# Reordering the start of a fused attention and deformable-convolution kernel, with a finer split at each image's border

## The chip, the cores and the metric

The kernel runs on one core of one Trainium2 chip. The metric is the device time of the whole program in microseconds, the median of the runs shown. One execution was also taken by the hardware profiler; every duration of one instruction below comes from that execution.

## The reference

The input `x` has 8 images of 256 channels by 64 by 64 pixels, all in 32-bit floats. Two residual layers follow each other, each on a group norm with 32 groups of 8 channels.

```
x = x + L0(gn(x))      # local attention over 3x3 windows
x = x + L1(gn(x))      # modulated deformable 3x3 convolution

L0: q, k, v = w_qkv @ x;  attn = softmax over the 9 neighbours of q.k (4 heads)
    kernel = w_kg @ (q, k, v) + b_kg              # 9 weights a pixel and head
    out = w_proj @ (alpha * sum(kernel * v_patch) + beta * sum(attn * v_patch))
L1: om = conv3x3(x, w_off) + b_off                # 18 offsets and 9 masks a pixel
    for each of 9 taps: sample x bilinearly at the shifted point (4 corners),
    times sigmoid(mask), then multiply by the tap's 256x256 weight and add up
```

## The kernel before

**Chunks, slots and halves.** An image is worked on in 8 chunks of 8 rows (512 pixels); 256 channels are two halves of 128 partitions. The kernel has two kinds of work. The *front* of an image is its first layer and the preparation of its second: `attention(b)` makes q, k, v, the logits, softmax, weighted sums and projection chunk by chunk, then `prepare(b)` norms the result, writes it to a table in DRAM whose row holds a pixel and its lower neighbour (`to_table`), and computes the offsets (`Offsets`: 18 products of 32 columns, four of them side by side, for one chunk), their transposes (`turn`) and from them row numbers and weights (`positions`). The *sampling* of an image then takes 72 slots, one for each chunk and tap. A slot has four blocks of 128 pixels. For each block GpSimd issues an indirect DMA (`gather`, line 1092) that brings 128 rows of 4 KB; ScalarE scales the first corner (`scale`, line 1108); VectorE adds the other three (`sum_corners`, line 1116, in pairs of blocks); TensorE transposes the blocks (line 1146), ScalarE copies them to SBUF (line 1149), and TensorE multiplies by the tap's weight (line 1171).

**What sets the order.** The instructions of TensorE, ScalarE, VectorE and GpSimd are written out by hand: they run in the order of the program text. The front is a Python generator, and each `next(steps)` writes out one step of it; 144 steps (`STEPS`) make an image. In the main loop each slot is issued in two halves, with one step of the next image's front after each half. So the first image's front runs with nothing beside it, the fronts of images 1 to 7 lie between the samplings of images 0 to 6, and the sampling of the last image has no front beside it. `STEPS_AHEAD = 12` says how far the front leads when sampling begins; the start-up code hands out these 12 steps one by one between the first gathers:

```
for n in range(4): next(steps, None)
for i in range(6): gather(i)
next(steps, None); scale(0); scale(1)
next(steps, None); sum_corners(0)
for i in range(6, LEAD, 2):        # LEAD = 16 blocks
    next(steps, None)
    ...                            # gathers 6 to 15, a few scales and sums between
next(steps, None)
```

**Buffers.** Gathered blocks have 10 buffers (`GATHERS`), and a gather waits until the sum has read the buffer's last block. Products of the front go through 4 PSUM buffers in turn (`psum_a`). So a product waits until ScalarE or VectorE has read what lies in its buffer; the logits' products (`products`, line 394) are read by `masked` on VectorE (line 407), and v's products follow them in the same four buffers.

**The start.** The first image's 8 chunks, `w_qkv` in two parts, and the small `w_kgT` are loaded by the queues of SP and ScalarE. TensorE makes from the last two the folded weight (`folded`, line 225), VectorE takes the statistics of each chunk (line 299) and collects them (line 192). Then `fold` scales the folded weight on VectorE (lines 237 and 244). The norm (`Norm`) has two steps: `means` is a product with `gmat` (line 197) and four small VectorE instructions, `ready` a second product (line 208), a square root on ScalarE, and two more. Only then can VectorE norm the chunk (`normed`, line 269) and TensorE make q (line 320).

**The border of two images.** At the end of `prepare(b)` the offsets of chunk 6 (`six`) are made in three parts, products 0 to 5, 6 to 11 and 12 to 17. The next image's `attention` begins with `means`, then `ready`, then its first jobs, of which the first is `turn(six)`.

Of the kernel before, what the change touches and what calls it, by code (L numbers as in the profile page):

```python
# [9 lines left out]
F32 = mybir.dt.float32  # L10
# [7 lines left out]
P = 128  # L18
C = 256
NT = C // P  # L20
# [6 lines left out]
NC = H // R  # L27
KK = 9
# [18 lines left out]
SUM_AHEAD = 6  # L47
SCALE_AHEAD = SUM_AHEAD + 2
GATHERS = 10
LEAD = SUM_AHEAD + GATHERS  # L50
STEPS = 2 * SLOTS
STEPS_AHEAD = 12

@with_exitstack
def preact_kernel(ctx: ExitStack, tc: tile.TileContext, a: dict, out: bass.AP):
# [30 lines left out]
    def load_chunk(b, c, queue=nc.sync):  # L88
        s = slice(c * N, (c + 1) * N)
        queue.dma_start(image[:, :, s], sources[b][:, :, s])  # L90
# [8 lines left out]
    gp = ctx.enter_context(tc.tile_pool(name="gp", bufs=GATHERS))  # L99
    w_qkv = [gp.tile([96, 4, C], F32, tag="g", name=f"w_qkv{i}") for i in range(2)]  # L100
    w_kgT = gp.tile([96, 8, KK], F32, tag="g", name="w_kgT")
    queues = nc.sync, nc.scalar
    for c in range(4):
        load_chunk(0, c, queues[c % 2])
    for i in range(2):
        queues[i].dma_start(w_qkv[i], a["w_qkv"][:, 4 * i : 4 * i + 4, :])
    nc.scalar.dma_start(w_kgT, a["w_kgT"])
    for c in range(4, NC):
        load_chunk(0, c, queues[c % 2])
    gmat = const_tile("gmat", [P, P])  # L110
    w_qkvT = const_tile("w_qkvT", [P, NT, 3 * C], nc.sync)
    alpha = const_tile("alpha", [P, 1])
# [68 lines left out]

    def psum_a(name):
        return ps_a.tile([P, 512], F32, tag="a", name=name)

    class Norm:

# [440 lines left out]
    def attention(b):  # L627

        xt = image
        first = b == 0  # L630
        jobs, due[:] = due[:], []
        gn = norm0[b]
        if b != 1:
            gn.means()
        stats = p2.tile([P, NT, NC, 6], F32, tag="stats", name=f"stats1_{b}")
        yield None
        gn = gn.gn if b == 1 else gn.ready()
        yield None
        xn = normed(xt, gn, 0, 2)
        for job in jobs[:1]:  # L640
            job()
        yield None
        d = added = None
        for c in range(NC):
            if c != 1:
                a_ = Attention(b, c, xn, stats)
                a_.q(0)
                if added:
                    added.second_stats()
                if c in (2, 5, 6, 7):  # L650
                    yield None
                a_.q(1)
                yield None if c == 4 else "quiet"
            else:
                a_ = follows
            ahead_of = c + 1 < NC
            at = 2 * (c % 2)
            a_.k(0)
            if ahead_of:
                xn = normed(xt, gn, c + 1, at, cts=(0,))  # L660
            yield None if ahead_of else "quiet"
            a_.k(1)
            if ahead_of:
                normed(xt, gn, c + 1, at, cts=(1,))
            if first:
                for n in (c - 1, c)[: 1 + (c == NC - 1)]:
                    if n >= 0:
                        first_stats(1, n)
            yield None if ahead_of else "quiet"
            if d and not first:  # L670
                d.keys(0)
            a_.products(0)
            for job in jobs[c - 1 : c] * (c in (2, 3)):
                job()
            yield None if c in (2, 3) else "quiet"
            a_.generated()
            a_.masked(0)
            yield None
            a_.products(1)
            a_.turned()  # L680
            yield "quiet"
            if d:
                d.weighted(0)
            else:
                a_.v(0)
            a_.masked(1)
            a_.summed()
            yield None
            a_.logits_1()
            a_.carry_k()  # L690
            if d:
                d.keys(1)
                d.carry_v()
                yield None
                a_.v(0)
                a_.logits_2()
                a_.softmax_1()
                yield None
                d.weighted(1)
                a_.twisted()  # L700
            else:
                a_.v(1)
                a_.logits_2()
                yield None
                a_.softmax_1()
                a_.twisted()
                follows = Attention(b, 1, xn, stats)
                follows.q(0)
            yield None
            if d:  # L710
                a_.v(1)
            else:
                follows.q(1)
            a_.softmax_2()
            a_.softmax_3()
            yield None
            if d:
                d.add(0, d.project(0))
                yield None
            a_.weights()  # L720
            if first and c == NC - 1:
                norm0[1].means()
            if d:
                d.add(1, d.project(1))
                added = d
            yield None
            a_.spread_weights()
            if first and c == NC - 1:
                norm0[1].ready()
            if first:  # L730
                a_.keys(0)
            yield None
            d = a_
        if not first:
            d.keys(0)
        added.second_stats()
        yield None
        d.weighted(0)
        yield "quiet"
        d.keys(1)  # L740
        yield "quiet"
        d.weighted(1)
        yield "quiet"
        if not first:
            later[0]()
        yield "quiet"
        d.add(0, d.project(0))
        d.add(1, d.project(1))
        d.second_stats()
        gn = Norm(stats, f"1_{b}")  # L750
        yield None
        if not first:
            later[1]()
        yield "quiet"
        gn.means()
        yield None
        gn.ready()
        yield gn.gn

    def prepare(b, gn):  # L760
# [199 lines left out]
        def turn(o):  # L960
            pairs[o.c // 2] = o.turned(o.c % 2)
# [11 lines left out]
        if b == 0:  # L973
            flat(1)
            order = (
                "T0 z2 x1 T1 z3 O0 T2 t z4 x2 O1 T3 t z5 p0 T4 z6 x3 O2 T5 t z7 x4 T6 O3 "
                "T7 t x5 O4 x6 t O5 x7 t p2 S0 S1 S2"
            )
            for job in order.split():
                kind, n = job[0], int(job[1:] or 0)  # L980
                if kind == "T":
                    to_table(n)
                elif kind == "z":
                    flat(n)
                elif kind == "x":
                    xn[n] = normed(xt, gn, n, n % 3, (n - 1) % 3)
                    for m in range(n - 1, n + (n == NC - 1)):
                        nc.gpsimd.tensor_copy(image[:, :, m * N : (m + 1) * N], second[m])
                elif kind == "O":
                    o = Offsets(n, xn[n])  # L990
                    o.all()
                elif kind == "t":
                    turn(o)
                elif kind == "p":
                    positions(n, pairs[n // 2], 2)
                elif n == 0:
                    six = Offsets(NC - 2, xn[NC - 2])
                    six.part(0, 6)
                elif n == 1:
                    six.part(6, 12)  # L1000
                else:
                    six.part(12, KK * NT)
            o = Offsets(NC - 1, xn[NC - 1])
            for n in range(2 * NC):
                yield
# [16 lines left out]
        if b > 0:  # L1022
# [15 lines left out]
                first_stats(b + 1, NC - 1)  # L1038
            o = Offsets(NC - 1, xn[NC - 1])
            yield  # L1040
            six.part(12, KK * NT)
        if not more:
            yield
            turn(six)
# [11 lines left out]
            return  # L1056
        later[:] = [o.first, o.rest, o.positions]
        due[:] = [
            lambda: turn(six),
            lambda: positions(4, pairs[2], 2),  # L1060
            lambda: positions(6, pairs[3]),
# [139 lines left out]
        mybir.EngineType.Pool,  # L1201
    }
    with tc.manual_schedule(engines=ordered):
        ps = folded()
        for c in range(NC):
            first_stats(0, c)
# [2 lines left out]
        for n in range(STEPS):  # L1209
            next(steps, None)  # L1210

        for n in range(4):
            next(steps, None)
        for i in range(6):
            gather(i)
        next(steps, None)
        scale(0)
        scale(1)
        next(steps, None)
        sum_corners(0)  # L1220
        for i in range(6, LEAD, 2):
            next(steps, None)
            if holds:
                nc.gpsimd.memset(holds.pop(), 0.0)
            if i == 8 or i == 12:
                sum_corners(i // 2 - 2)
            gather(i)
            gather(i + 1)
            if i in (6, 10, 14):
                scale(i // 2 - 1)  # L1230
                scale(i // 2)
        next(steps, None)
        done = STEPS + STEPS_AHEAD
        last = None
        for n in range(B * SLOTS + 1):
            late, last = last, None
# [2 lines left out]
            for m in range(NT):  # L1239
# [14 lines left out]
                        stored(*last, slice(m, m + 1))  # L1254

                h = NT * n + m + 1
                goal = h * STEPS
                while (done - STEPS - STEPS_AHEAD) * STEPS < goal:
                    state["quiet"] = next(steps, True)
                    done += 1  # L1260
                if n < B * SLOTS:
# [77 lines left out]
```

## Time and profile before

| what | value |
|---|---|
| runs shown | 4606.46, 4612.72, 4614.89 us; median 4612.72 |
| profiled execution: its time, its span | 4635.28 us, 4633.3 us |
| TensorE busy, matmul records | 4480.2 us (97%), 25344 |
| VectorE, ScalarE, GpSimd busy | 4130.8 us (89%), 2514.2 us (54%), 2783.1 us (60%) |
| gathers: records, share of the DMA engines | 2304, 74.4% |

The profiled execution took 22.6 us more than the median of the runs; differences between steps are read inside it. A 32-bit product of 128 by 128 with 512 columns appears as two matmul records. In a row of the timeline the first number is the start in microseconds from the span's start, the second is the time from the group's start to its end, and the bracket says how long the engine had been idle before it and on what it waited. In a row of the windows each engine has its busy microseconds within the stretch; PEclk is the granted TensorE clock as a share of full speed, then come the share of the DMA engines and GB/s.

### The profile page before, as it was taken

The numbers are of one execution on the slowest core, as the hardware profiler recorded it, in microseconds if no ns is written. First come the engines' busy times: TensorE is split into PE (matmuls) and PEld (weight loads), VectorE is DVE, ScalarE is ACT, GpSimd is POOL, SyncE is SP. The second block draws the span as 40 slices with busy tenths as digits, with TensorE's granted clock in tenths as the row PEclk, the third lists the DMA queues.
The fourth block names the chain that finished last, engine by engine and source line by source line (L and its number), as shares of the span: only waits on it lengthen the run. The fifth ranks groups of instructions, "written<-read, shape, count | busy, mean of one in ns | idle before, by whom it ended". The sixth has DMA issues, their size and how long they took to land.

```text
span 4633.3 us, 77608 instructions
## 1 busy us (share of the span) xinstructions
PE 4480.2 (97%) x25344; PEld 2332.3 (50%) x25344; DVE 4130.8 (89%) x10183; ACT 2514.2 (54%) x5280; POOL 2783.1 (60%) x2850
## 2 busy tenths in 40 slices
PE   8989999999999999999999999999999999998888
PEld 4445554555545555455554555555554555543344
DVE  6669999999999999999989999999999999988777
ACT  3345556555565555555555555655556555554444
POOL 0046655666555665566655665556655666568887
PEclk9999999999999999999999999999999999999999
DMA  4078889888998899988899888998899888899998
GB/s 143 28 230 294 304 312 368 314 301 303 310 385 297 294 312 320 369 295 306 301 338 331 298 307 311 354 331 297 299 315 373 296 287 302 296 335 333 352 336 317
DMA packets 445761, 1412.46 MB, mean 305 GB/s; under 512 B 46430, under 2 KB 63070, under 8 KB 445228
## 3 DMA queue, kind: packets, MB, share of 16 engines
q0 software_dynamic: 331776, 1208.11, 74.4%
q1 hardware_dynamic: 111836, 196.82, 11.8%
q8 instruction: 199, 3.26, 0.3%
q10 hardware_dynamic: 1744, 2.59, 0.2%
q14 instruction: 206, 1.69, 0.1%
HBM read 1275.97 MB, written 131.36 MB: 304 GB/s over the span
## 4 chain that ended last, share of the span: by engine, by line
PE 86%; DVE 4%; DMA 4%; issue 2%; POOL 2%; ACT 1%; another core or an unknown queue 0%; POOLq 0%; DVEq 0%; ACTq 0%; SPq 0%
PE po L1171 38%; PE pt L1146 10%; PE psk L351 5%; PE psq L320 5%; PE proj L602 5%; PE psv L351 5%; PE om L838 5%; PE av L586 3%; DVE s L1116 3%; PE vk L568 2%; PE qk L394 2%; DMA g<-table,idx 2%; PE wk L542 2%; PE gen L437 1%; DMA x<-in_x_dram 1%
## 5 line engine op out<-in xcount | busy, mean ns | idle before, releaser
L1092 POOL DMA_INDIRECT g<-table,idx x2304 | 2670.7, 1159 | 1352.4 <-DVE s L1116 409.1
L1116 DVE SCALAR_TENSOR_TENSOR s<-g,wt,s 128x256 f32<-128x256 f32 x6912 | 2822.9, 479 | 185.8 <-ACT s L1108 127.2
L1171 PE MATMUL po<-vt,w_conv 128*128 128x512 f32 x4608 | 2198.1, 602 | 0.4 <-issue 0.3
L1171 PEld LDWEIGHTS po<-vt,w_conv 128*128 128x128 f32 x4608 | 813.9, 192 | 774.8 <-issue 765.4
L1108 ACT ACTIVATE s<-g,wt 128x256 f32<-128x256 f32 x2304 | 1053.5, 511 | 204.8 <-DMA g<-table,idx 133.1
L1149 ACT COPY vt<-pt 128x512 f32<-128x512 f32 x1152 | 618.2, 589 | 456.5 <-PE pt L1146 330.8
L1146 PE MATMUL pt<-ident,s 128*128 128x128 f32 x4608 | 646.1, 280 | 76.4 <-ACT vt L1149 32.5
L1146 PEld LDWEIGHTS pt<-ident,s 128*128 128x128 f32 x4608 | 527.2, 142 | 340.9 <-issue 197.8
L838 PE MATMUL om<-xn,w_off 128*32 128x512 f32 (+1 forms) x2560 | 272.4, 553 | 0.0
L351 PE MATMUL psv<-xn,w_qkvT 128*128 128x512 f32 (+1 forms) x576 | 251.5, 564 | 3.7 <-issue 2.8
L351 PE MATMUL psk<-xn,w_qkvT 128*128 128x512 f32 (+1 forms) x576 | 246.8, 557 | 0.0
L320 PE MATMUL psq<-xn,w_qkvT 128*128 128x512 f32 x512 | 240.6, 600 | 2.8 <-issue 2.5
L602 PE MATMUL proj<-acc,w_projT 128*128 128x512 f32 x512 | 239.6, 593 | 0.7 <-ACT acc L593 0.7
L328 ACT COPY q<-psq 128x512 f32<-128x512 f32 x128 | 74.8, 586 | 234.5 <-PE psq L320 228.4
L407 DVE TENSOR_TENSOR qk<-qk,near_k 128x400 f32<-128x400 f32 x256 | 134.8, 569 | 73.7 <-PE qk L394 36.8
L593 ACT COPY acc<-av 128x512 f32<-128x512 f32 x128 | 74.8, 584 | 227.9 <-PE pt L1146 164.0
L362 ACT COPY k<-psk 128x512 f32<-128x512 f32 (+1 forms) x144 | 79.1, 551 | 202.3 <-PE psk L351 179.7
L586 PEld LDWEIGHTS av<-wk,vk 100*64 100x64 f32 x4096 | 133.0, 137 | 107.2 <-issue 64.1
L838 PEld LDWEIGHTS om<-xn,w_off 128*32 128x32 f32 x2560 | 75.0, 109 | 207.7 <-issue 201.3
L573 ACT COPY vk<-vk 100x512 f32<-100x512 f32 x256 | 138.3, 592 | 62.2 <-PE vk L568 52.8
L550 DVE TENSOR_TENSOR wk<-wk,near 100x512 f32<-100x512 f32 x256 | 158.7, 682 | 12.9 <-PE wk L542 12.8
L586 PE MATMUL av<-wk,vk 100*64 100x64 f32 x4096 | 154.4, 225 | 12.1 <-issue 11.4
(107 smaller groups left out, 3387.6 us busy)
## 6 DMA issues: line engine op xcount, KB each, us to landing
table<-ts SPq DMA_DIRECT2D x128, 384.0 KB
g<-table,idx POOLq DMA_INDIRECT x2304
x<-x SPq DMA_DIRECT2D x56, 512.0 KB
r<-x SPq DMA_DIRECT2D x56, 512.0 KB
out_dram<-r SPq DMA_DIRECT2D x56, 512.0 KB
x<-in_x_dram SPq DMA_DIRECT2D x52, 512.0 KB
table<-ts SPq DMA_DIRECT2D x128, 128.0 KB
second<-in_x_dram SPq DMA_DIRECT2D x8, 512.0 KB
```

Of the source, the lines that this page charges most:

```text
L320: nc.tensor.matmul(ps, w_qkvT[:, ct, m * P : (m + 1) * P], window(self.xn, ct, 4), start=(ct == 0), stop=(ct == NT - 1),)
L351: nc.tensor.matmul(ps[:, : (hi - lo) * W], w_qkvT[:, ct, o : o + P], self.xn[:, ct, lo:hi, 1 : W + 1], start=(ct == 0), stop=(ct == NT - 1),)
L550: nc.vector.tensor_mul(wk.rearrange("p (t n) -> p t n", n=T * T), ps[:NK].rearrange("p (t n) -> p t n", n=T * T), near.unsqueeze(1).to_bro ...
L586: nc.tensor.matmul(av[64 * h : 64 * h + 64, g, t * T * T : (t + 1) * T * T], self.vk[:, t, o : o + 64], self.wk[2 * g + h][:, i * n + t * ...
L602: nc.tensor.matmul(ps, w_projT[:, ct, m * P : (m + 1) * P], self.acc[:, ct].rearrange("p (t y x) -> p y t x", y=T, x=T), start=(ct == 0), ...
L838: nc.tensor.matmul(self.ps[32 * g : 32 * g + 32, cols], w_off[:, ct, k, :], window(self.xn, ct, k)[:, ys], start=(n < 4), stop=(tail >= 0),)
L1092: nc.gpsimd.indirect_dma_start(out=g, out_offset=None, in_=tables[b % 2], in_offset=bass.IndirectOffsetOnAxis(ap=found[b, c][0][:, j, k : ...
L1108: nc.scalar.activation(s, g[:, 0:C], AF.Copy, scale=w[:, 0:1])
L1116: nc.vector.scalar_tensor_tensor(s, g[:, q * C : (q + 1) * C], w[:, q : q + 1], s, ALU.mult, ALU.add)
L1146: nc.tensor.transpose(pt[ct][:, j, :], s[:, ct * P : (ct + 1) * P], ident)
L1149: nc.scalar.copy(v[:, ct, :], pt[ct].rearrange("p b n -> p (b n)"))
L1171: nc.tensor.matmul(po[m], w_conv[:, ct, k, m * P : (m + 1) * P], v[:, ct, :], start=(k == 0 and ct == 0), stop=(b + 1 < B and k == KK - 1 ...
```

## The change

Three things are changed, and one of them has two places.

1. **The start's loads.** `w_kgT` is moved from seventh to third in the order of loads, and both parts of `w_qkv` are put on ScalarE's queue. The order of the first chunks over the two queues changes with that, and the last two chunks no longer have the first loads of other constants ahead of them.
2. **Products of zeros.** A tile `warm` of zeros is multiplied into a PSUM buffer whose content nobody reads: 9 products of 512 columns ahead of `folded`, and 2 between the end of the first image's attention and its second norm.
3. **The lead at the start of sampling.** Sampling begins when the front is 8 steps ahead (`STEPS_FIRST`) instead of 12. Gathers 0 to 9 are issued in a row after the fourth step, without the small memset that held gather 6 back; scales and sums of the first six blocks follow, with four steps between them. In the main loop four extra steps are handed out over the first 144 halves (after halves 1, 37, 73 and 109), so that the lead is 12 from then on.
4. **The border.** For all images but the last, the last three of the 18 offset products of chunk 6, with the copy that follows, are issued after the next image's `means` instead of before it.

```diff
+STEPS_FIRST = 7 + 1
...
-    for c in range(4):
-        load_chunk(0, c, queues[c % 2])
+    load_chunk(0, 0)
+    load_chunk(0, 1, nc.scalar)
+    nc.scalar.dma_start(w_kgT, a["w_kgT"])
+    load_chunk(0, 2)
     for i in range(2):
-        queues[i].dma_start(w_qkv[i], a["w_qkv"][:, 4 * i : 4 * i + 4, :])
-    nc.scalar.dma_start(w_kgT, a["w_kgT"])
-    for c in range(4, NC):
-        load_chunk(0, c, queues[c % 2])
+        nc.scalar.dma_start(w_qkv[i], a["w_qkv"][:, 4 * i : 4 * i + 4, :])
+    load_chunk(0, 3)
+    load_chunk(0, 5)
+    load_chunk(0, 4, nc.scalar)
+    load_chunk(0, 7)
+    load_chunk(0, 6, nc.scalar)
...
+    warm = const.tile([P, 512], F32, name="warm")
+    nc.vector.memset(warm, 0.0)
+    warming = psum_a("warm")
+
+    def kept_warm(n, size=512):
+        for i in range(n):
+            nc.tensor.matmul(
+                warming[:, :size], warm[:, :P], warm[:, :size], start=True, stop=True
+            )
...
+        part, jobs = jobs[:1], jobs[1:]
         gn = norm0[b]
         if b != 1:
             gn.means()
+        for job in part:
+            job()
...
         gn = Norm(stats, f"1_{b}")
+        if first:
+            kept_warm(2)
...
-            six.part(12, KK * NT)
+            six.part(12, 15 if more else KK * NT)
...
         due[:] = [
+            lambda: six.part(15, KK * NT),
             lambda: turn(six),
...
     with tc.manual_schedule(engines=ordered):
+        kept_warm(9)
         ps = folded()
...
-        for n in range(4):
+        for n in range(STEPS_FIRST - 4):
             next(steps, None)
-        for i in range(6):
+        for i in range(GATHERS):
             gather(i)
-        next(steps, None)
-        scale(0)
-        scale(1)
-        next(steps, None)
-        sum_corners(0)
-        for i in range(6, LEAD, 2):
-            next(steps, None)
-            if holds:
-                nc.gpsimd.memset(holds.pop(), 0.0)
-            if i == 8 or i == 12:
-                sum_corners(i // 2 - 2)
-            gather(i)
-            gather(i + 1)
-            if i in (6, 10, 14):
-                scale(i // 2 - 1)
-                scale(i // 2)
-        next(steps, None)
-        done = STEPS + STEPS_AHEAD
+        for i in range(0, SUM_AHEAD, 2):
+            if i == 0:
+                scale(0)
+                scale(1)
+            scale(i + 2)
+            scale(i + 3)
+            sum_corners(i)
+            gather(i + GATHERS)
+            gather(i + GATHERS + 1)
+            for n in range(2 if i == 0 else 1):
+                next(steps, None)
+        done = STEPS + STEPS_FIRST
...
-                goal = h * STEPS
-                while (done - STEPS - STEPS_AHEAD) * STEPS < goal:
+                goal = h * STEPS + min(h, STEPS) * (STEPS_AHEAD - STEPS_FIRST)
+                while (done - STEPS - STEPS_FIRST) * STEPS < goal:
```

More of the change, by code (lines that the diff above doesn't have):

```diff
@@ L101, in preact_kernel @@
     w_kgT = gp.tile([96, 8, KK], F32, tag="g", name="w_kgT")
-    queues = nc.sync, nc.scalar
-    for c in range(4):
-        load_chunk(0, c, queues[c % 2])
+    load_chunk(0, 0)
+    load_chunk(0, 1, nc.scalar)
+    nc.scalar.dma_start(w_kgT, a["w_kgT"])
+    load_chunk(0, 2)
     for i in range(2):
-        queues[i].dma_start(w_qkv[i], a["w_qkv"][:, 4 * i : 4 * i + 4, :])
-    nc.scalar.dma_start(w_kgT, a["w_kgT"])
-    for c in range(4, NC):
-        load_chunk(0, c, queues[c % 2])
+        nc.scalar.dma_start(w_qkv[i], a["w_qkv"][:, 4 * i : 4 * i + 4, :])
[4 more added lines that the diff above has]
+    load_chunk(0, 6, nc.scalar)
     gmat = const_tile("gmat", [P, P])
@@ L1001, in prepare @@
                 else:
-                    six.part(12, KK * NT)
+                    six.part(12, 15)
             o = Offsets(NC - 1, xn[NC - 1])
@@ L1040, in prepare @@
             yield
-            six.part(12, KK * NT)
+            six.part(12, 15 if more else KK * NT)
         if not more:
```

## The prediction

> **What bounds the kernel now.** I read the page first, then the windows, then the timelines of the three places that the change touches.
>
> ```profile
> span 4633.3 us, 77608 instructions
> PE 4480.2 (97%) x25344; PEld 2332.3 (50%) x25344; DVE 4130.8 (89%) x10183; ACT 2514.2 (54%) x5280; POOL 2783.1 (60%) x2850
> ...
> 0.00:27.00 27.00, 8.14 (x37) 8.00 (x38) 13.92 (x35) 1.54 (x2) 7.13 (x10) 1.00 0.84 262
> 224.00:231.00 7.00, 1.86 (x8) 0.93 (x6) 4.98 (x17) 1.89 (x4) 0.04 (x1) 0.81 0.20 76
> 272.00:340.00 68.00, 57.41 (x357) 30.79 (x347) 52.01 (x128) 28.73 (x64) 38.68 (x37) 0.90 0.72 246
> 340.00:720.00 380.00, 378.91 (x2151) 201.36 (x2150) 353.18 (x847) 209.94 (x451) 232.22 (x230) 1.00 0.88 301
> ```
>
> TensorE is the bound: from 340 to 720 us it is idle for 1.1 of 380 us. Work that only changes place there gains nothing. Time can come from three holes: 0 to 27 (18.9 us idle), 224 to 231 (5.1 us), 272 to 340 (10.6 us, at 0.90 of the clock). What is saved in them moves everything behind forward, since the order behind them is the same from half 109 on.
>
> **The start.** TensorE waits for `w_kgT`, VectorE for the last chunk, and both chains meet at the norm:
>
> ```profile
> 16.73 7.00 PE L225 MATMUL eff<-w_kgT,w_qkv 96*128 96x9 f32 x32 [16.73 <-DMA w_kgT<-in_w_kgT_dram]
> 20.61 1.28 DVE L299 BATCH_NORM_STATS2 stats<-x 128x6 f32<-128x512 f32 x2 [1.67 <-DMA x<-in_x_dram]
> 21.81 0.58 DVE L192 BATCH_NORM_AGGREGATE mv<-stats 128x2 f32<-128x48 f32 x2
> 23.57 0.57 PE L197 MATMUL gn<-mv,gmat 128*128 128x2 f32 x2
> 24.22 0.15 DVE L199 COPY gn<-gn 128x2 f32<-128x2 f32 x1
> 26.86 5.40 PE L320 MATMUL psq<-xn,w_qkvT 128*128 128x512 f32 x8 [1.26 <-issue]
> ```
>
> The statistics are collected at 22.39, but the product with `gmat` stands behind the fold's 32 records and starts at 23.57. With `w_kgT` and `w_qkv` early the fold is done sooner: 1.1 us, the lower end unless the zeros are late. The last chunk: 5659 KB are queued ahead of its landing (8 chunks of 512, 2 times 384, 27, and `w_qkvT` with 768), landed 19.9 us after the first issue at 0.74. With `w_qkvT` behind it, 4891 KB are ahead, in proportion 17.2 us: 2.7 us sooner. But the last two chunks then land together and two more statistics (1.28) are left to do, so 1.4 us. The sum is 1.4 + 1.1 = 2.5 us; upper end 2.7 + 1.1 = 3.8. The fold's three VectorE instructions (0.54) lie beside the product with `gmat`; without that cover they cost 0.5.
>
> The nine zero products cost nothing while TensorE waits for loads: at the records' 0.43 us warm and 0.86 cold (q's first records stand 0.86 apart, eight later ones take 3.46) they are 7.7 to 15.5 us from about 2.7 us, and the fold's 7.0 us follow. If all of it runs cold it ends at 25.2 instead of 23.7: the lower end is a loss of 1.5. I take 2.5.
>
> A rule of the Trainium skill speaks against the new order of queues. Its first page, Trainium Kernel Development and Optimization (Key Constraints), says that DMAs of several queues share the same 16 engines and that a second queue saves only issue time. By that alone the gain would be only what the bytes ahead give, which is how the sum was made.
>
> **Two products of zeros at the second norm.**
>
> ```profile
> 226.94 0.38 PE L197 MATMUL gn<-mv,gmat 128*128 128x2 f32 x2 [2.48 <-DVE mv L192]
> 228.16 0.49 PE L208 MATMUL gv<-gnd,gmat 128*128 128x2 f32 x2 [0.84 <-DVE gnd L203]
> 230.24 0.47 PE L791 MATMUL ptab<-ident,z 128*128 128x128 f32 x1 [1.60 <-ACT z L773]
> 230.95 3.46 PE L791 MATMUL ptab<-ident,z 128*128 128x128 f32 x15 [0.23 <-ACT z L773]
> ```
>
> TensorE has little to do from 224.46 to 230.24, the granted clock falls to 0.81 in this window, and the next records are slow: 15 transposes take 3.46 where 8 take 1.09 later, and the first offsets 4.44 instead of 4.07. That is worth 2.1 us. The two products (1.72 us) fit into the first wait of 2.48 and delay nobody. They leave 226.2 to 230.24, 4.0 us with 0.9 us of work. The upper end is 2.1 us, the lower 0; I take 0.5, near to nothing, because the wait that is left is longer than the 2.8 us blank at 289 (below) after which the clock also fell.
>
> The skill's page TensorE: Matmul & The Clock Gate (Part 1) says that an idle window of about 3.4 us halves the clock. By it the 4.0 us left are usually enough, and the gain is 0 more often than 2.1.
>
> **Eight steps ahead.** The timeline of 272 to 340:
>
> ```profile
> 272.72 1.11 POOL L1092 DMA_INDIRECT g<-table,idx  x1 [4.69 <-issue]
> 283.65 2.47 DVE L1116 SCALAR_TENSOR_TENSOR s<-g,wt,s 128x256 f32<-128x256 f32 x6 [4.99 <-ACT s L1108]
> 291.79 3.33 PE L351 MATMUL psv<-xn,w_qkvT 128*128 128x512 f32 x8 [2.82 <-issue]
> 307.30 1.09 PE L529 MATMUL w<-ident,wts 128*128 128x128 f32 x4 [3.02 <-ACT s L1108]
> 334.30 1.91 PE L1146 MATMUL pt<-ident,s 128*128 128x128 f32 x8
> ```
>
> The row at 334.30 is the fifth slot's transposes. In the new order I place the work by its rows: gathers 1.25 us each from 272.72, as before; scales 0 to 3 on ScalarE at 281.0, after q's copies; sums 2.46 a pair; masking 1.06; halves of q, k, v and products 1.72; a slot's transposes 0.87. VectorE: sum 0 to 284.0, norming 1.13, sums 2 and 4 to 290.05, masking to 291.1, sum 6 to 293.6, masking to 294.65. TensorE: `generated` ends at 287.0, the first transposes wait for sum 2 until 287.6, the second logits for the first masking until 290.6, v for the second masking until 294.15. From there v (3.87), transposes, two products and two q halves end at 305.8; the next slot's transposes and product at 308.4; the weights' transposes wait for VectorE's softmax until 309.6. Products, spreading, the fourth transposes, and two products and two k halves end at 320.6. The old order has done 4.2 us more of the front by its fifth transposes (vk 0.97, two logits 1.72, `generated` 1.01, its transposes 0.5), so 324.8 compares with 334.30: 9.5 us, the upper end.
>
> This assumes that nothing is late without reason. Before, three blanks are not explained by work: 2.82 at 289, 3.02 at 304, and 2.0 between 330.8 and 333.4 ("issue" again), in a stretch where the gathers fill the DMA engines. Around them the clock of the windows of 10 us is 0.66 (from 290), 0.84 (300), 0.99 (310) and 0.83 (330): 6.8 us lost. All three back with their clock cost 7.8 + 6.8 = 14.6: lower end 9.5 - 14.6 = -5.1. I take one blank, 2.8, since the new order cannot answer for them: **6.7 us**. The ten gathers in a row fill GpSimd until 285.2; nothing else is queued there. ScalarE's scales 4 to 7 stand before `gs`; if their gathers are late, the transposes of `gs` and v wait behind them.
>
> **The border.** At the first of seven borders nothing stands between, so TensorE's order stays; six are like this one:
>
> ```profile
> 816.55 2.06 DVE L1116 SCALAR_TENSOR_TENSOR s<-g,wt,s 128x256 f32<-128x256 f32 x5
> 818.52 0.15 DVE L199 COPY gn<-gn 128x2 f32<-128x2 f32 x1
> 819.32 0.38 PE L208 MATMUL gv<-gnd,gmat 128*128 128x2 f32 x2 [0.76 <-DVE gnd L202]
> ```
>
> The moved products are about 0.65 us (3 of 18 at 4.0 us). They fill the 0.76 only if the second product keeps its time; but VectorE comes to the copy straight from sums, so TensorE is merely earlier before and waits as long. The moved copy of 0.69 on ScalarE stands before the table load for the root; VectorE is in sums then. Ends: 0 and 6 times 0.65 = 3.9, a loss of 0.4 a border if the root's delay is seen; I take 0.3 in all.
>
> **The sum.** 2.5 + 0.5 + 6.7 + 0.3 = 10.0 us from 4635.28, so 4625.3 in the profiled execution, 22.6 above the median; carried to the median 4612.72 - 10.0 = **4602.7 us**. About 0.2% (9.2 us) is what a measurement of this kernel can tell from no change, and 4603.5 is that bound.
>
> **Rivals.**
>
> *The blanks come back* (0.18). The burst of gathers is the same load. For it: "issue" and late releases at 289 to 297 with the DMA engines busy. Against it: the pause of GpSimd between gather 5 and 6 goes. With two blanks and their clock (about 9) the lead is worth nothing: 2.5 + 0.5 + 0.3 = 3.3, 4609.4, no change.
>
> *Slower: halves with two steps* (0.14). From 300 to 720 us the front is 8 to 11 steps ahead, and halves 37, 73 and 109 carry two steps. VectorE is 93% busy there, so sums can come late. The nearest price is the border at 2481.6, where TensorE waited 3.0 and 0.9 us and the window of 10 us around it lost 3.4 us of clock (0.66): 7.3 us. Three of these less the 10.0 make +11.9, 4624.6; it decides for slower than before from two such stalls, for a measurable loss from three. Against it: a chunk of the front has some 14 steps and a chunk of sampling 18 halves, so nearly every pairing occurs before, with 1.1 us idle.
>
> *The change does not do what it says*: zeros that don't keep the clock and a border that fills nothing. It is nearly in the sum; without those two parts 9.2 us, 4603.5, on the bound.
>
> **How the numbers follow.** The schedule holds with 0.68; its own range is 4594 to 4609 (gains of 19 to 4: all upper ends, or a second blank). Of it 0.50 lies beyond the bound. So faster 0.50, within 0.2% 0.18 + 0.18 = 0.36, slower 0.14. The range 4592 to 4620 takes in the upper ends and part of the slower case.
>
> **What would show it.** Right: q's first product near 24.3; the first transposes of the fifth slot some 9 us earlier, counted with the same front work; no wait above 2 us between 285 and 335; PE idle of about 1 us in the 380 us after. Wrong: `w_kgT` early but the last chunk still at 20.6; waits of 3 us with a half clock at 290 to 310; VectorE named as releaser of transposes between 340 and 720.

## The result and the profile after

The changed kernel took 4636.04 us against 4609.59 of the kernel before on the same chip (medians): the ratio is 1.0056, with a 95% interval of 1.0044 to 1.0069. It is slower by about 26 us, where 10 us less were forecast. In a second measurement (r1_after, below) the ratio was 1.0036 (1.0022 to 1.0050), 16 us. Both intervals lie above 1. The medians give 26 and 16 us and the intervals reach from 10 to 32 us, so the size is not known closer.

The profiled execution of before had been 22.6 us above its median and that of after (4628.52) was below its own, so the two spans must not be set against each other; what follows compares places inside the executions. First the page's span and engines, and the windows at the same stretches as before, with one more from 27 to 224 us, the first image's attention:

```profile
span 4626.6 us, 77646 instructions
PE 4509.6 (97%) x25366; PEld 2333.7 (50%) x25366; DVE 4133.5 (89%) x10183; ACT 2522.3 (55%) x5280; POOL 2780.0 (60%) x2849
...
0.00:27.00 27.00, 18.05 (x57) 10.35 (x58) 15.95 (x40) 1.55 (x2) 7.13 (x10) 0.85 0.85 269
27.00:224.00 197.00, 188.41 (x1356) 96.61 (x1354) 116.44 (x218) 68.52 (x139) 0.00 (x0) 0.92 0.17 58
224.00:231.00 7.00, 6.92 (x100) 4.40 (x98) 5.72 (x11) 2.86 (x6) 0.00 (x0) 1.00 0.01 2
272.00:340.00 68.00, 57.74 (x411) 27.82 (x410) 45.18 (x113) 32.33 (x65) 30.10 (x29) 0.95 0.87 261
340.00:720.00 380.00, 379.04 (x2172) 201.51 (x2170) 356.09 (x853) 210.06 (x451) 239.27 (x229) 1.00 0.87 299
```

The same stretch of the kernel before, which the prediction did not look at:

```profile
27.00:224.00 197.00, 192.12 (x1588) 101.30 (x1588) 133.48 (x257) 78.30 (x159) 0.00 (x0) 0.99 0.17 62
```

That row shows where the time goes. The busy time hardly moves, 192.12 to 188.41, but only 1356 matmul records were done in the same 197 us instead of 1588, and the clock granted fell from 0.99 to 0.92. The window 224 to 231, a hole before, is now full (6.92), because the attention isn't over by then: the second norm's first product starts at 254.30 instead of 226.94, 27.4 us later, although q's first product is 2.2 us *earlier*.

One chunk of the attention, from one row of spreading products (`wk`) to the next, lasts 27.2 us instead of 23.4. TensorE's timeline where one chunk ends and the next begins, before:

```profile
95.20 1.12 PE L542 MATMUL wk<-wsb,spread 9*100 9x512 f32 x8
...
118.61 1.12 PE L542 MATMUL wk<-wsb,spread 9*100 9x512 f32 x8
119.66 1.08 PE L568 MATMUL vk<-ident,v 128*100 128x128 f32 x8
120.58 3.63 PE L320 MATMUL psq<-xn,w_qkvT 128*128 128x512 f32 x8
```

and after, with the row for this tile from the list of waits of the whole execution (us in total, times, longest); before has no such row:

```profile
101.26 1.11 PE L556 MATMUL wk<-wsb,spread 9*100 9x512 f32 x6
103.14 1.10 PE L556 MATMUL wk<-wsb,spread 9*100 9x512 f32 x2 [0.77 <-DVE wk L564]
104.17 1.71 PE L582 MATMUL vk<-ident,v 128*100 128x128 f32 x8
105.67 4.70 PE L334 MATMUL psq<-xn,w_qkvT 128*128 128x512 f32 x8
...
128.50 1.11 PE L556 MATMUL wk<-wsb,spread 9*100 9x512 f32 x6
...
PE wk L556 <- DVE wk L564: 6.2, 8, 0.8
```

A chunk's four spreading products, one for each head, ran side by side before (8 records in 1.12 us). After, three run side by side and the fourth waits 0.77 us for VectorE to read the first, then runs by itself: from the first to what follows them 2.91 us instead of 1.05. What follows is slow as well: q's eight records take 4.70 us, where they took 3.63 before.

**The cause.** `warming` is asked for once from the 4 PSUM buffers that the front's products use in turn, and is written at two places: at the start and, by the two products of zeros, at the second norm. Between the two it isn't free. So from 2.73 to 253.5 us the front has 3 buffers, and the fourth product of each chunk waits for the buffer of the first. The releaser in the row at 103.14 says so (line 564 is VectorE's reading of a spreading product), and the first two experiments test it.

### The profile page after: what moved, and what is told of

Read it like the earlier page. It is cut to its first block, busy times and chain, and to the rows that moved or that the text cites. A ratio compares the mean times of both kernels' runs of the same rounds, so it can differ in the third digit from the quotient of the medians.

```text
span 4626.6 us, 77646 instructions
## 1 busy us (share of the span) xinstructions
PE 4509.6 (97%) x25366; PEld 2333.7 (50%) x25366; DVE 4133.5 (89%) x10183; ACT 2522.3 (55%) x5280; POOL 2780.0 (60%) x2849
## 4 chain that ended last, share of the span: by engine, by line
PE 88%; POOL 4%; DMA 4%; DVE 2%; issue 1%; ACT 1%; SPq 0%; another core or an unknown queue 0%; POOLq 0%; ACTq 0%; DVEq 0%
PE po L1191 38%; PE pt L1166 10%; PE om L857 5%; PE psv L365 5%; PE psq L334 5%; PE psk L365 5%; PE proj L616 5%; PE av L600 3%; DMA g<-table,idx 3%; POOL g L1112 3%; PE vk L582 3%; PE qk L408 2%; PE wk L556 2%; PE gen L451 1%; PE ptab L810 1%
```

## The experiments

Theory: the held buffer costs 25 to 30 us, in all eight chunks of the first image, and the rest of the change brings about what the prediction said. Rivals: the new lead of 8 steps costs it (the prediction's slower case), or the new order of loads does, or the zeros' own time and what they do to the clock. Kernels under one heading below were run on one chip and share the runs of before; medians of different headings are on different chips and are not compared (before: 4588.43, 4610.04, 4610.91).

### First chip: hold the buffer alone, and give it back

**e2_hold**, the kernel before with nothing but the buffer held: two tiny products of zeros.

```diff
+    warm = const.tile([P, 512], F32, name="warm")
+    nc.vector.memset(warm, 0.0)
+    warming = psum_a("warm")
...
         gn = Norm(stats, f"1_{b}")
+        if first:
+            kept_warm(1, 2)
...
     with tc.manual_schedule(engines=ordered):
+        kept_warm(1, 2)
         ps = folded()
```

> The kernel before, with the tile of zeros and its PSUM buffer held from the start to the first image's second norm, but only one product of 2 columns at each end; loads, lead and border as before. Theory (held buffer: the zeros' tile takes one of the four rotating PSUM buffers for the whole of the first image's attention, so that the fourth spreading product waits for VectorE in each of 8 chunks): the chunk of the first image's attention takes 25 to 27.5 us instead of 23.4, the second norm comes 20 to 30 us later, and the time is 20 to 30 us above the kernel before. Rival (the clock's windows fall differently because of the zero products and the earlier start): a chunk stays at 23.4 and the time within 5 us of before. Rival (the lead or the burst of gathers is what costs): no change, within 5 us.

Measured: 4617.57 against 4588.43, ratio 1.0066 (1.0052 to 1.0080): 29 us slower, and none of the change's loads, lead, border or large products is in it. Its windows and waits of the same stretch are those of the changed kernel:

```profile
27.00:224.00 197.00, 188.38 (x1348) 95.88 (x1352) 118.09 (x223) 68.45 (x139) 0.00 (x0) 0.94 0.17 59
...
PE wk L552 <- DVE wk L560: 6.2, 8, 0.8
```

**e1_fresh**, the whole change, but with a buffer of its own for each group of zeros, so that it is free again after them.

```diff
-    warming = psum_a("warm")
-
     def kept_warm(n, size=512):
+        warming = psum_a("warm")
         for i in range(n):
```

> The changed kernel, with all its parts, but each call of the zero products takes a PSUM buffer of its own and gives it back at once. Theory (held buffer): the chunk is 23.4 us again, the time is 26 to 36 us below the changed kernel, so 0 to 10 us below the kernel before. Rival (clock windows, zeros): the chunks stay long in some executions, time still 15 to 30 us above before. Rival (lead and gathers): time still 15 to 30 us above before.

Measured: 4575.86, ratio 0.9971 (0.9959 to 0.9983): 12.6 us *faster* than before. A line moved turns the sign. The wait is gone, chunks last 23.4 us, and TensorE isn't idle from 300 to 720 us:

```profile
27.00:224.00 197.00, 192.62 (x1582) 102.66 (x1581) 131.05 (x251) 78.39 (x159) 0.00 (x0) 0.96 0.18 61
300.00:340.00 40.00, 40.00 (x239) 21.42 (x239) 38.49 (x94) 24.42 (x53) 27.61 (x24) 1.00 0.80 269
340.00:720.00 380.00, 380.00 (x2179) 201.96 (x2178) 354.34 (x852) 210.32 (x451) 226.70 (x228) 1.00 0.88 304
```

**e8_no_zeros**, the change without `warm`, `warming` and both groups of zeros; loads, lead and border are kept.

```diff
-        if first:
-            kept_warm(2)
...
-        kept_warm(9)
         ps = folded()
```

> The changed kernel without any product of zeros: loads, lead and border as changed. Theory (held buffer): as with fresh buffers, 0 to 10 us below the kernel before; against it by the worth of the zeros alone, some 0 to 3 us. Rival (lead and gathers): 15 to 30 us above before. Rival (clock windows through the zeros): below before by 5 to 10 us, as the theory, and only the run with fresh buffers tells these two apart.

Measured: 4578.53, ratio 0.9979 (0.9970 to 0.9988): 9.9 us faster. So the zeros, which were to bring a gain, bring 2.7 us by the medians when their buffer is given back (1.4 us on the third chip), and the intervals overlap both times.

**e3_lead**, the kernel before with the lead of 8 steps alone (the last part of the change's diff, nothing else).

```diff
+STEPS_FIRST = 7 + 1
...
-        for n in range(4):
+        for n in range(STEPS_FIRST - 4):
             next(steps, None)
-        for i in range(6):
+        for i in range(GATHERS):
             gather(i)
...
-                while (done - STEPS - STEPS_AHEAD) * STEPS < goal:
+                goal = h * STEPS + min(h, STEPS) * (STEPS_AHEAD - STEPS_FIRST)
+                while (done - STEPS - STEPS_FIRST) * STEPS < goal:
```

> The kernel before with the lead of 8 steps alone. Theory (held buffer; the lead is worth what the prediction's schedule gave): 3 to 9 us below the kernel before. Rival (lead and gathers cost): 15 to 30 us above. In the profile the fifth slot's transposes come 4 to 9 us earlier, counted with the same work of the front.

Measured: 4583.95, ratio 0.9990 (0.9981 to 0.9998): 4.5 us faster, with an interval of 0.9 to 8.7. In its timeline TensorE has one idle time of about 2 us at the start of sampling, and the fifth slot's transposes start at 322.30:

```profile
229.81 0.38 PE L198 MATMUL gn<-mv,gmat 128*128 128x2 f32 x2 [2.48 <-DVE mv L193]
...
292.58 1.40 PE L395 MATMUL qk<-k,q 64*64 64x100 f32 x30 [2.09 <-DVE qk L408]
...
322.30 1.03 PE L1147 MATMUL pt<-ident,s 128*128 128x128 f32 x8
```

### Second chip: the mechanism's inside, and the small parts

**e9_fill**, the changed kernel with one product of zeros more ahead of each fourth spreading product of the first image. The buffer stays held, so the fourth waits for the first's reading as ever; only TensorE isn't idle then. It tells the wait apart from the clock.

```diff
             for h in range(HEADS):
+                if self.b == 0 and h == HEADS - 1:
+                    kept_warm(1)
                 ps = psum_a(f"wk_{self.u}_{h}")
```

> The changed kernel with its held buffer, and one more product of zeros (0.86 us warm) ahead of the fourth spreading product in each of the first image's 8 chunks, where TensorE waits 0.77 us for VectorE. Theory (of the 3.9 us that a chunk has lost, some 1.9 are the fourth product standing apart from the other three, and some 2.0 are the window at half clock that follows the wait): the clock stays full, a chunk takes 25.2 to 25.8 us instead of 27.3, the time is 10 to 16 us below the changed kernel, so 10 to 16 us above the kernel before. Rival (the wait alone costs, the half clock costs nothing that the path sees): a chunk takes 27 to 28 us and the time is 24 to 30 us above before.

Measured: 4619.95, ratio 1.0016 (1.0006 to 1.0026), 10 us slower than before. A chunk lasts 25.8 us, between 23.4 and 27.2. Stretches of 3.4 us around one chunk's spreading, in the changed kernel

```profile
101.30:104.70 3.40, 2.63 (x13) 0.99 (x13) 3.00 (x5) 0.00 (x0) 0.00 (x0) 0.96 0.40 154
104.70:108.10 3.40, 3.40 (x10) 2.01 (x9) 3.40 (x7) 1.17 (x2) 0.00 (x0) 0.53 0.00 1
```

and in e9_fill, with the timeline there:

```profile
101.30:104.70 3.40, 3.40 (x17) 1.27 (x12) 2.85 (x6) 0.05 (x1) 0.00 (x0) 1.00 0.41 154
104.70:108.10 3.40, 3.40 (x12) 1.70 (x10) 3.40 (x7) 1.61 (x3) 0.00 (x0) 1.00 0.02 5
```

```profile
100.85 1.11 PE L558 MATMUL wk<-wsb,spread 9*100 9x512 f32 x6
101.89 1.12 PE L195 MATMUL warm<-warm 128*128 128x512 f32 x2
102.94 1.10 PE L558 MATMUL wk<-wsb,spread 9*100 9x512 f32 x2
```

A blank of 0.77 us is followed by 3.4 us at half the clock (0.53); with the blank filled the clock stays at 1.00. That is 27.2 - 25.8 = 1.4 us of the 3.8 lost in a chunk. The other 2.4 us are the wait and the lost company: the fourth product's own 1.03 us, the 1.05 us in which it waits (here filled with zeros), and 0.3 us in smaller places. The product of zeros is both work in the blank and work of 128 rows, so this run doesn't say which of the two keeps the clock.

**e4_loads**, the kernel before with the new order of loads alone.

```diff
+    load_chunk(0, 0)
+    load_chunk(0, 1, nc.scalar)
     nc.scalar.dma_start(w_kgT, a["w_kgT"])
+    load_chunk(0, 2)
+    for i in range(2):
+        nc.scalar.dma_start(w_qkv[i], a["w_qkv"][:, 4 * i : 4 * i + 4, :])
+    load_chunk(0, 3)
+    load_chunk(0, 5)
+    load_chunk(0, 4, nc.scalar)
+    load_chunk(0, 7)
+    load_chunk(0, 6, nc.scalar)
```

> The kernel before with the new order of loads alone. Theory (prediction's step): the first product of q starts 2.0 to 3.0 us earlier than at 26.86, and the time is 1 to 4 us below the kernel before. Rival (the fold was not in the way, or the last chunk still lands at 20.6): q at 26 to 27, no change.

Measured: 4608.15, ratio 0.9996 (0.9984 to 1.0007): 1.9 us less, not told from nothing. In its profile q starts 1.1 us sooner, where 2.0 to 3.0 were expected:

```profile
22.48 0.59 PE L200 MATMUL gn<-mv,gmat 128*128 128x2 f32 x2 [4.64 <-DMA turn_x<-in_turn_x_dram]
23.90 0.59 PE L211 MATMUL gv<-gnd,gmat 128*128 128x2 f32 x2 [0.84 <-DVE gnd L206]
25.76 4.44 PE L323 MATMUL psq<-xn,w_qkvT 128*128 128x512 f32 x5 [1.27 <-issue]
```

All of it comes from the fold that is out of the way. The statistics are collected at 21.84, no sooner than before (21.81). The nine other executions with the new order of loads collect them at 20.14 to 20.91, so the last chunk does land sooner with it, but not every time.

**e7_border**, the kernel before with the border alone.

```diff
+        part, jobs = jobs[:1], jobs[1:]
...
-                    six.part(12, KK * NT)
+                    six.part(12, 15)
...
         due[:] = [
+            lambda: six.part(15, KK * NT),
```

> The kernel before with the finer split at the border alone. Theory (VectorE is in sums at the border, so TensorE only waits elsewhere): within 2 us of the kernel before. Rival (the moved products fill the wait of 0.8 us at each of six borders): 3 to 5 us below before, and the waits for the second product of the norm are gone from the borders.

Measured: 4610.13, ratio 0.9999 (0.9990 to 1.0007): no difference is seen.

**e10_more_zeros**, e1_fresh with one more product of zeros after `means` and two more after `ready`, so that TensorE's waits in the second norm are filled for the greater part.

```diff
         gn.means()
+        if first:
+            kept_warm(1)
         yield None
         gn.ready()
+        if first:
+            kept_warm(2)
```

> The changed kernel with fresh buffers for the zeros, and at the first image's second norm one more product between its two products and two more behind the second, so that TensorE has work in all three waits there. Theory (the two products of the change leave a hole in which the clock still falls): the clock stays full through the second norm, the first 16 transposes of the table take 2.2 us instead of 3.5 to 4, and the time is 1 to 3 us below the run with fresh buffers alone, 13 to 16 us below the kernel before. Rival (ScalarE sets the pace there): transposes faster, time the same as with fresh buffers.

Measured: 4602.19, ratio 0.9983 (0.9973 to 0.9993). That is 7.9 us below before, where 13 to 16 were expected. The clock holds now: the first eight transposes take their 1.09 us at once.

```profile
225.51 1.96 PE L195 MATMUL warm<-warm 128*128 128x512 f32 x4
227.31 0.27 PE L814 MATMUL ptab<-ident,z 128*128 128x128 f32 x1
227.96 1.09 PE L814 MATMUL ptab<-ident,z 128*128 128x128 f32 x8 [0.37 <-ACT z L796]
229.37 0.98 PE L814 MATMUL ptab<-ident,z 128*128 128x128 f32 x7 [0.32 <-ACT z L796]
```

### Third chip: the four versions side by side

**r1_after** is the changed kernel again, **r2_fresh** is e1_fresh, **r3_more_zeros** is e10_more_zeros, **r4_no_zeros** is e8_no_zeros; the diffs are those above. They were to tell which version is the best, and how large the change's loss is on the chip of the repaired ones.

> The changed kernel again, beside three of its mended forms on one chip. Theory (held buffer): 22 to 30 us above the kernel before, a chunk of the first image's attention 27.2 us long in the profile, with one window at half clock in each. Rival (the eight windows of the first execution were a chance of the clock): some chunks of 25 to 26 us, and 10 to 20 us above before.

> The changed kernel with a fresh PSUM buffer for each call of the zeros, again: 8 to 14 us below the kernel before, 34 to 40 us below the changed kernel.

> Fresh buffers and five zero products at the second norm instead of two. Theory (the clock stays full there): 1 to 3 us below the run with fresh buffers of this call. Rival (the last products stand in front of the first transposes, or ScalarE sets the pace): the same as that run, within 2 us, or up to 2 us above.

> The changed kernel without zeros. Theory (nine zeros ahead of the fold and two at the norm are worth little): within 3 us of the run with fresh buffers. Rival (they are worth what the earlier call's medians differ by): 2 to 4 us above it.

Measured, against 4610.91: r1_after 4626.97 (1.0036, 1.0022 to 1.0050), r2_fresh 4601.19 (0.9979, 0.9969 to 0.9989), r3_more_zeros 4600.07 (0.9979, 0.9968 to 0.9990), r4_no_zeros 4602.57 (0.9983, 0.9974 to 0.9992). From r1 to r2, one moved line, is 25.8 us (34 to 40 were expected), and between the starts of their second norms lie 26.4 us:

```profile
255.51 0.38 PE L211 MATMUL gn<-mv,gmat 128*128 128x2 f32 x2 [0.76 <-DVE mv L206]
...
229.10 0.38 PE L211 MATMUL gn<-mv,gmat 128*128 128x2 f32 x2 [0.76 <-DVE mv L206]
```

In the same way e2_hold's second norm starts at 255.68, 28.7 us after that of before, and it is 29 us slower. The three repaired versions are 8 to 11 us below the kernel before, and which of them is best was not resolved: within 2.5 us they are the same. On the first chip e2_hold's 29 us less e1_fresh's 12.6 give the changed kernel a loss of 16 us, which is what r1_after has on the third. The first measurement's 26 us (20 to 32) is more than that, and the rest is not explained.

r1_after also shows the clock's share without any filling. After its wait at 211.05 no half clock follows, and that chunk takes 25.8 us, where the five chunks before it take 27.2 to 27.3:

```profile
211.05 1.10 PE L556 MATMUL wk<-wsb,spread 9*100 9x512 f32 x2 [0.77 <-DVE wk L564]
...
236.84 1.58 PE L556 MATMUL wk<-wsb,spread 9*100 9x512 f32 x2 [0.77 <-DVE wk L564]
```

## Why the prediction was wrong

**The step that failed** is the price of the zeros: "The nine zero products cost nothing while TensorE waits for loads", and of the two at the second norm that they "fit into the first wait of 2.48 and delay nobody". Both sentences price the products' time on TensorE. Neither asks what the tile that they write costs while nobody writes it. The term that is missing from the sum is the held buffer, 26 us by r1 and r2 and 29 us by e2_hold, against a sum of 10.0. None of the rivals had it either: the slower side was reached by a mechanism that was not on the list. The rows to price it were in the trace of before. A fourth product that no longer runs beside the others adds a second 1.05 us, and it can't start until VectorE has read the first, for which the trace of before has this row (line 550, the same stretch):

```profile
119.75 2.48 DVE L550 TENSOR_TENSOR wk<-wk,near 100x512 f32<-100x512 f32 x4 [0.34 <-PE wk L542]
```

Four readings in 2.48 us are 0.62 each; eight chunks of 1.05 + 0.62 give 13 us, which alone undoes the gain (an estimate from these rows; the part without the clock measured 2.4 us a chunk, 19 us). No row that the prediction shows would have priced the clock's 1.4 us a chunk.

**Without that term the sum held.** 10.0 us were forecast; e1_fresh, the change with the buffer given back, measured 12.6 and 9.7 us on two chips. It is the total that is borne out, and no term by itself: measured alone, the parts add up to 7.7 to 9.0 us (loads 1.9, lead 4.5, border -0.1, zeros 1.4 or 2.7), and each has an interval of some 4 to 5 us either way. The parts, by the prediction's steps:

*The start*, 2.5 us predicted, 2.2 in the changed kernel's timeline:

```profile
2.73 11.03 PE L195 MATMUL warm<-warm 128*128 128x512 f32 x18 [2.73 <-DVE warm L190]
13.60 3.64 PE L239 MATMUL eff<-w_kgT,w_qkv 96*128 96x9 f32 x32
20.56 0.59 DVE L206 BATCH_NORM_AGGREGATE mv<-stats 128x2 f32<-128x48 f32 x2
21.20 0.59 PE L211 MATMUL gn<-mv,gmat 128*128 128x2 f32 x2 [3.96 <-DVE mv L206]
24.63 6.02 PE L334 MATMUL psq<-xn,w_qkvT 128*128 128x512 f32 x8 [1.42 <-DVE xn L283]
```

The statistics are collected at 20.56 instead of 21.81, 1.25 us sooner (1.4 predicted), and the product with `gmat` follows them by 0.64 instead of 1.76, 1.1 us (1.1 predicted): the fold is out of the way at 17.2. q starts at 24.63 where 24.3 was to be seen. In the other executions with the whole new start q starts between 24.17 and 24.98. The nine products neither delay the fold's end nor speed the start: without them (e8_no_zeros) the fold starts at 10.52 and takes 7.29 us, with them it starts at 13.60 and takes 3.64. It ends at 17.8 and 17.2, and the product with `gmat` waits in both for the statistics. As device time the start is not settled: e4_loads' interval reaches from 7 us less to 3 us more.

*The two products at the second norm*, 0.5 us "near to nothing": right in the timeline, and for the reason given. They end, and then

```profile
251.66 1.88 PE L195 MATMUL warm<-warm 128*128 128x512 f32 x4
254.30 0.38 PE L211 MATMUL gn<-mv,gmat 128*128 128x2 f32 x2 [0.76 <-DVE mv L206]
257.56 0.33 PE L810 MATMUL ptab<-ident,z 128*128 128x128 f32 x1 [1.60 <-ACT z L792]
258.27 3.40 PE L810 MATMUL ptab<-ident,z 128*128 128x128 f32 x15 [0.38 <-ACT z L792]
```

the 15 transposes take 3.40 us, against 3.46 before. What was left idle, 4.0 us with 0.7 of work, was enough for the clock to fall. e10_more_zeros shows what it takes to hold it, and that holding it saves 1.1 us in the timeline (3.04 us for these 16 where e8_no_zeros takes 4.17), too little to be seen in the time (r3_more_zeros and r2_fresh differ by 1.1 us).

*Eight steps ahead*, 6.7 us predicted, 4.5 (0.9 to 8.7) measured by e3_lead. The placing of the work was right. From the second norm's first product (226.94) to the fifth slot's transposes (334.30) before took 107.4 us; e3_lead takes 322.30 - 229.81 = 92.5. That is 14.9 us, 10.7 after the 4.2 of front work that are put off, where 9.5 was the upper end. The wait of 2.09 us in it is no unexplained blank: the schedule had the second logits wait for the masking from about 288.5 to 290.6. But this is one execution, and a good one. The blanks that the new order "cannot answer for" came back in others. r2_fresh is the same kernel as e1_fresh, which has none of them, and r4_no_zeros the same as e8_no_zeros:

```profile
289.75 0.94 PE L408 MATMUL qk<-k,q 64*64 64x100 f32 x16 [2.34 <-issue]
...
287.73 0.95 PE L398 MATMUL qk<-k,q 64*64 64x100 f32 x16 [5.81 <-issue]
```

By the same count e3_lead, e8_no_zeros and e1_fresh take 92.5, 92.7 and 93.9 us, and r3_more_zeros, r4_no_zeros, r2_fresh and e10_more_zeros 96.8, 97.2, 99.0 and 100.6; with the old lead it is 106.2 to 107.4 (e4_loads, e7_border, before). Against the mean of those three, 106.8, and after the 4.2, that is a gain of 2.0 to 10.1 us, 6.5 in the mean of the seven. So 6.7 was a fair price, the allowance for a blank was needed, and the first rival's mechanism is real, though with it the repaired versions on the third chip are still 8 to 11 us faster. Waits came in the changed kernel itself too (1.65 us, "issue", at 316 and 2.41 us for VectorE at 324).

*The border*, 0.3 us predicted, is near to nothing: e7_border's ratio of 0.9999 goes with it, and its interval (4.6 us less to 3.2 us more) doesn't resolve the ends.

*The slower rival*, halves with two steps and VectorE late from 300 to 720 us, is refuted: from 340 to 720 us TensorE is idle for 1.0 of 380 us in the changed kernel and for 0.00 in e1_fresh (1.8 in r1_after, 1.6 in r2_fresh), against 1.1 before. The range, 4592 to 4620, left out 4636.

On the clock the prediction drew on the Trainium skill's page TensorE: Matmul & The Clock Gate (Part 1) for one long idle window. The same part, in its section A second HAM failure mode: psum-queue depth-cycling, also describes a second way to lose the clock, for a kernel in bf16: TensorE idles briefly between groups of products as they cycle through PSUM banks, and often enough for the clock to swing between half and full. This case's trace agrees in kind, with 0.77 us idle followed by 3.4 us at 0.53, so an idle window of 3.4 us was not needed here. The passage bears on the clock's part of the loss alone, 1.4 of the 3.8 us a chunk.

## What to carry to other kernels

A tile taken from a rotating pool and used at two distant places takes its buffer out of the rotation for all that lies between, so cost an added tile by its lifetime first and by its instructions second: count the buffers that the busiest group between needs at once (here four heads, four buffers). Compare on what each instruction waits before and after; one product in each loop body that comes to wait for another engine can outweigh all the terms at the program's edges, since it is multiplied by the loop. Dummy work that is to fill a wait should ask for its buffer where it is issued.

## What the runs showed of the hardware

Three things were not expected. **A wait of 0.77 us can cost 3.4 us at half the clock, chunk after chunk.** In the changed kernel the fourth spreading products start at 75.90, 103.14, 130.38, 157.61, 184.86 and 212.11 us, and stretches at half the clock start at 77.15, 104.45, 131.76, 159.07, 186.37 and 213.68, each about 3.41 us long; e2_hold has six as well. These stretches come 27.3 us apart, 8 times 3.41, and that seems to say that the chunk is drawn to the clock's own period. The numbers say otherwise: the products come 27.24 us apart, so the chunk slides by some 0.06 us against the stretches each time, and 27.2 is also what a chunk without the half clock (25.8 in r1_after) and the 1.4 us lost to it give. Nor does every such wait cost the clock: r1_after has the same 0.77 us at 211.05 and no half clock behind it. Where the wait falls against the clock's stretches may decide; this was not tested.

**A stretch that is 77% busy can still lose the clock.** Before the half clock, TensorE was busy for 2.63 of 3.40 us, but mostly with products of 9 rows. The fold's products of 9 columns are also thin. In e8_no_zeros they take 7.29 us back to back with no speeding up, and 3.64 us when large zero products ran ahead of them:

```profile
10.52 7.29 PE L229 MATMUL eff<-w_kgT,w_qkv 96*128 96x9 f32 x32 [10.52 <-DMA w_qkv<-in_w_qkv_dram]
```

The profile's clock column doesn't help there: it gives 1.00 from 0 to 27 us in e8_no_zeros and in before, although q's first records stand 0.86 us apart in before, twice the later 0.43. Whether thin products count as little activity, or the 0.77 us of idle time decides, is open.

**The medians of the same kernel differ from chip to chip** by nearly as much as the whole effect: before took 4588.43 us on one and 4610.91 on another. Only ratios against runs on the same chip carry anything here.
